# Score-weight loads in two steps, with two small loads moved and a fixed order on SyncE

## The chip, the cores and the metric

The kernel runs on one core of one Trainium2 chip. The metric is the device time of one execution in microseconds; the time shown for a kernel is the median of its runs.

## The reference

There are 128 graphs of 128 nodes with 512 features each, all in float32. Two layers follow each other; each normalizes its input, applies a ReLU, runs a graph layer and adds the result to its input.

```python
# layer 0: graph attention with K = 3 hops
h  = relu(layernorm(x))
Xw = h @ Wv + bv
e  = leaky_relu((Xw @ aw[:d])[:, None, :] + (Xw @ aw[d:])[:, :, None] + ab, 0.2)
t  = adj * exp(e);  t = t / (t.sum(-1, keepdims=True) + 1e-12)
H = 0;  Xk = h
for k in range(3):
    H = H + Xk @ Wk[k] + bk[k];  Xk = t @ Xk
x = x + relu(H)
# layer 1: one attention weight for each node
h = relu(layernorm(x))
q, k = split(h @ Wqk);  v = h @ Wv1
w = (q * (adj @ (k * mask))).sum(-1) * mask / sqrt(512)
x = x + softmax(w, axis=1)[:, :, None] * v
```

## The kernel before

The core works on pairs of graphs, 64 pairs in all. A loop over the pairs does layer 0 and the normalization of layer 1; a second loop over groups of two pairs does layer 1. The large matrix products are cut by Strassen's scheme into seven products of half-size blocks, so TensorE multiplies sums of blocks that VectorE has formed. Ahead of the first loop stands a setup of about 30 us, and the change is there.

**Setup.** The scores of layer 1 need q and k only through one product of them, so the kernel forms the score matrix Wq Wk^T once. The score weights `wqk` (512 x 1024, 2 MB) are loaded into `wqk_sb`, which lies in the tile `tl` (the profile names it `tl`). They come in eight pieces of 256 KB. `oh` is the half of the columns, first or second, of both the q and the k part; `ch` and `c` name the four chunks of 128 rows. Pieces with `c = 0` are issued by SyncE and those with `c = 1` by ScalarE (lines 144 to 150). Then SyncE issues the first pair of graphs (`load_x(0)`, tile `xg`), the attention weights `wv0` (in tile `t10`, named `t`), the second pair, and the three hop weights `wk` (tiles `w2` and `r10`, named `w` and `r`; lines 181 to 187).

GpSimd issues the small loads: the attention vector `awj`, the node mask `nm`, and two parts of the hop biases into `bkj` (lines 155 to 158). It then makes `ident`, the identity that transposes need. A one-element copy `gate` that reads the last piece of the score weights (line 183) holds back the other small loads `bvc`, `awc` and `ab_bc`; a second one that reads `wk[2]` holds back the adjacency loads (`load_adj`, tiles `ag` and `agb`).

TensorE starts with warm-up products on `ones` (`warm`, `warm_whole`, lines 770 to 772), whose results nobody reads. `weights_transposed(ch, oh, banks)` transposes two pieces into two PSUM banks, and ScalarE and VectorE copy them to `wqt` and `wkt`. `score_matrix(f, oh)` multiplies those. TensorE's order is written out by hand: transposes (0, 0), transposes (1, 0), three warm-up products, score matrix (0, 0), transposes (0, 1), masks, score matrix (1, 0), transposes (1, 1), and the rest of the score matrix with the transposes of the first graphs between. The first layer-0 product, `y2(0)`, follows.

VectorE, meanwhile, spreads the attention vector (`aw_bc`), takes the statistics of the first pair (`statistics(xg[0])`: `st`, `mv`, `r`, `rs`), forms the bias columns from `bkj` (`bias_columns`, tile `bkt`), multiplies `wv0` by the attention vector (`attention_columns`, tile `junk`), combines the weights (`combine`) and forms the block sums of the left operand (`left_sums`, tile `sx`).

**Order.** A planner puts the instructions of each engine in order and makes the semaphores for data dependences. `tc.issue_after(ins)`, and the helpers `behind` and `ordered` on it, add an edge of order alone: on `ins`'s engine, what is traced in the block comes later than `ins`, without a wait for its end. `ordered` chains all of TensorE's work.

Of the kernel before, what the change touches and what calls it, by code (L numbers as in the profile page):

```python
# [16 lines left out]
def kernel(  # L17
# [25 lines left out]
    nc = tc.nc  # L43
    B, N, D = x.shape
    K = wk.shape[0]
    P = 128
    DC = D // P
    HC = DC // 2
    HD = D // 2
    G = 2  # L50
    S32 = 32
    Q = P // S32
# [24 lines left out]
    done = {}  # L77

    a1, b1, c1, e1, a2, b2, c2, e2 = (psum.tile([P, D], FP, name=n) for n in
                                      ("a1", "b1", "c1", "e1", "a2", "b2", "c2", "e2"))  # L80
    set1, set2 = (a1, b1, c1, e1), (a2, b2, c2, e2)

    def behind(what, op, *args, **how):

        with tc.issue_after(done[what]):
            return op(*args, **how)  # L86

    def ordered(op, *args, **how):

        with tc.issue_after(done["mm"]):  # L90
            done["mm"] = op(*args, **how).ins  # L91

    def bcast(ap, offset, n):

        return bass.AP(tensor=ap.tensor, offset=ap.offset + offset, ap=[[0, P], [1, n]])

    xg, ag, agb = {}, {}, {}

    def load_x(p, queue=nc.sync):
        xg[p] = loads.tile([P, G, D], FP, name="xg")  # L100
        queue.dma_start(xg[p], x[p * G:(p + 1) * G].rearrange("b n d -> n b d"))

    def load_adj(p):

        s = slice(p * G, (p + 1) * G)
        ag[p] = loads.tile([P, G, N], FP, name="ag", bufs=3)
        nc.sync.dma_start(ag[p], adj[s].rearrange("b n m -> n b m"))
        agb[p] = loads.tile([P, G, Q, S32], FP, name="agb", bufs=2)
        v = adj[s].rearrange("g (q b) (c i) -> c b (g q) i", b=S32, i=S32)
        for c in range(Q):  # L110
            nc.gpsimd.dma_start(agb[p][c * S32:(c + 1) * S32].rearrange("p g q i -> p (g q) i"), v[c])  # L111
# [18 lines left out]
    wqk_sb = tl.rearrange("p t c o -> p (t c o)").rearrange("p (c o) -> p c o", c=DC)  # L130
# [5 lines left out]
    bkj = setup.tile([P, 2, S32], FP, name="bkj")  # L136
# [4 lines left out]
    awc = setup.tile([P, 2, DC], FP, name="awc")  # L141
    bvc = setup.tile([P, DC], FP, name="bvc")

    for oh in range(2):
        for ch in range(2):
            for c in range(HC):
                at = ch * HC + c
                (nc.scalar if c else nc.sync).dma_start(
                    wqk_sb[:, at].rearrange("p (a o) -> p a o", a=2)[:, :, oh * HD:(oh + 1) * HD],
                    wqk[at * P:(at + 1) * P].rearrange("p (a o) -> p a o", a=2)[:, :, oh * HD:(oh + 1) * HD])  # L150
    load_x(0)
    def blocks32(ap, offset, times, n):
        return bass.AP(tensor=ap.tensor, offset=ap.offset + offset, ap=[[0, times], [S32, n], [1, S32]])

    nc.gpsimd.dma_start(awj, blocks32(aw, 0, Q, S32))
    nc.gpsimd.dma_start(nm, nodemask)
    nc.gpsimd.dma_start(bkj[:, 0], blocks32(bk, 0, Q, S32))
    nc.gpsimd.dma_start(bkj[:, 1], blocks32(bk, 2 * D, 2 * Q, D // S32))

    ident = const.tile([P, P], FP, name="ident")  # L160
    make_identity(nc, ident)
# [20 lines left out]
    weights0 = [(wv0_sb, wv0), (r2[:, :, 1:1 + D], wk[2])] + [(r10[:, :, k], wk[1 - k]) for k in range(2)]  # L182
    done["gate"] = nc.gpsimd.tensor_copy(gate, wqk_sb[:, DC - 1, D - 1:D]).ins
    for dst, w in weights0:
        nc.sync.dma_start(dst, w.rearrange("(f p) o -> p f o", p=P))
        if dst is wv0_sb:
            load_x(1)
    with tc.issue_after(done["gate"]):
        nc.gpsimd.dma_start(bvc, bv0.rearrange("(p c) -> p c", c=DC))
        nc.gpsimd.dma_start(awc, aw.rearrange("(a p c) o -> p a (c o)", a=2, c=DC))  # L190
        done["gate"] = nc.gpsimd.dma_start(ab_bc, bcast(ab, 0, 1)).ins
        done["gate"] = nc.gpsimd.tensor_copy(gate, r2[:, DC - 1, D:1 + D]).ins
    load_x(2)

    def spread(dst, col):
# [39 lines left out]
    def warm(times, bank, start=True):  # L235

        for _ in range(times):
            with tc.issue_after(done["mm"]) if "mm" in done else ExitStack():
                done["mm"] = nc.tensor.matmul(bank[:, :P], ones, ones, start=start, stop=True,  # L239
                                              skip_group_check=True).ins  # L240
# [62 lines left out]
    def weights_transposed(ch, oh, banks):  # L303

        for a, bank in enumerate(banks):
            pt = bank.rearrange("p (k n) -> p k n", n=P)
            for c in range(HC):
                for o in range(HC):
                    at = a * D + (oh * HC + o) * P
                    ordered(nc.tensor.transpose, pt[:, o * HC + c if a else c * HC + o, :],  # L310
                            wqk_sb[:, ch * HC + c, at:at + P], ident)
            if a:
                on = "wq" if oh else "wk"
                done[on] = behind(on, nc.scalar.copy if oh else nc.vector.tensor_copy,
                                    wkt[:, oh * HC:(oh + 1) * HC, ch * HD:(ch + 1) * HD],
                                    bank.rearrange("p (o n) -> p o n", o=HC)).ins
            else:
                done["wq"] = behind("wq", nc.scalar.copy,
                                    wqt[:, oh * HC:(oh + 1) * HC].rearrange("p o f c a -> p (o f) c a")[
                                        :, :, ch * HC:(ch + 1) * HC],  # L320
                                    bank.rearrange("p (c o a) -> p o c a", c=HC, a=S32)).ins
# [450 lines left out]
    warm_whole(c2)  # L772
    done["warm"] = done["wk"] = done["wq"] = done["mm"]
    weights_transposed(0, 0, (a2, e2))
    weights_transposed(1, 0, (c1, e1))
    warm(3, b2, False)
    attention_vector_columns()
# [21 lines left out]
    for p in range(2):  # L799
        behind("gate", load_adj, p)  # L800
# [24 lines left out]
    with tc.issue_after(done["hv"]):  # L825
        load_x(3)
        load_adj(2)

    for p in range(NP):
# [4 lines left out]
        elif FIRST <= p < LAST:  # L834
            o, i = divmod(p - FIRST, 4)
# [31 lines left out]
        if LAST < p <= LAST + len(PIECES):  # L867
            o, i = PIECES[p - LAST - 1]
# [45 lines left out]
        if p + 3 < NP:  # L914
            load_adj(p + 3)
# [537 lines left out]
```

## Time and profile before

| quantity | value |
|---|---|
| time, median of 3 runs | 2204.94 us (2204.85 to 2206.91) |
| time of the profiled execution | 2207.55 us |
| its span in the profile | 2205.8 us |
| TensorE busy | 2196.1 us (100%) |
| VectorE, ScalarE, GpSimd busy | 77%, 56%, 35% |
| mean granted TensorE clock | 0.999 |
| moved by DMA | 503.14 MB, mean 228 GB/s |

The span is the time between the first and the last instruction in the profile; the execution's own time is 1.75 us longer. Busy time of TensorE is modelled and pipelined, so 100% says that it hardly ever waits, not that it runs at its peak. PE is TensorE's matrix product, PEld its weight load, DVE VectorE, ACT ScalarE, POOL GpSimd and SP SyncE; a name with a q, such as SPq, is the engine's issue of DMAs. A note in brackets gives the idle time ahead of an instruction and what ended it.

### The profile page before, as it was taken

To read this page: it belongs to the slowest core of one execution; us is meant where nothing else is said; L and a number is where in the kernel's file an instruction comes from. 1 tells how busy PE (TensorE), PEld (TensorE's weight loads), DVE (VectorE), ACT (ScalarE), POOL (GpSimd) and SP (SyncE) were. 2 spreads that over 40 slices of the span, in tenths; PEclk is the share of its full clock that TensorE was granted. 3 is DMA by queue.
4 is the path that set the end of the run, shared out by engine and by line. 5 is a ranking of instruction groups with operands and counts; after the bars stand their busy time and mean duration, and the time that the engine had idled before them with its cause. 6 is when DMAs were issued, how large, how long until landed. Compare 5 with 4: busy or idle time off the path is not lost.

```text
span 2205.8 us, 29518 instructions
## 1 busy us (share of the span) xinstructions
PE 2196.1 (100%) x8113; PEld 1534.7 (70%) x8113; DVE 1697.7 (77%) x4542; ACT 1233.4 (56%) x2856; POOL 778.1 (35%) x951
## 2 busy tenths in 40 slices
PE   9999999999999999999999999999999999999998
PEld 5666666665666666566666666688788878887886
DVE  6778788777878877877877777588777777777777
ACT  4555555555555455555545554466666666666665
POOL 2222222222222222222222222255545554555454
PEclk9999999999999999999999999999999999999999
DMA  6788778777878888887878887868887888787877
GB/s 212 203 227 242 221 237 239 236 245 226 247 226 241 233 237 239 223 246 224 243 220 242 232 231 208 285 181 218 237 224 229 214 236 225 224 218 231 231 212 182
DMA packets 433693, 503.14 MB, mean 228 GB/s; under 512 B 101880, under 2 KB 282104, under 8 KB 429560
## 3 DMA queue, kind: packets, MB, share of 16 engines
q1 hardware_dynamic: 381016, 375.72, 55.9%
q0 software_dynamic: 51136, 123.97, 22.7%
q10 hardware_dynamic: 1376, 1.57, 0.2%
q8 instruction: 65, 1.06, 0.2%
q14 instruction: 100, 0.82, 0.1%
HBM read 287.17 MB, written 213.94 MB: 227 GB/s over the span
## 4 chain that ended last, share of the span: by engine, by line
PE 99%; DVE 0%; DMA 0%; issue 0%; DVEq 0%; ACT 0%
PE a L91 29%; PE c L91 26%; PE b L91 26%; PE e L91 17%; DMA tl<-in_L_gnn_Wqk_dram 0%; DVE c L728 0%; DVE h L728 0%; PE b L239 0%; DVE junk L728 0%; ACT L114 0%; DVEq L1449 0%; PE a L197 0%; DVE x L397 0%; DVE z L86 0%; DVE peak L728 0%
## 5 line engine op out<-in xcount | busy, mean ns | idle before, releaser
L728 POOL TENSOR_TENSOR c<-s,c 128x512 f32<-128x512 f32 (+1 forms) x186 | 201.0, 1093 | 250.6 <-DVE s L728 245.5
L483 POOL DMA_DIRECT2D fd<-fw x124 | 78.4, 636 | 491.6 <-DVE fw L471 459.0
L111 POOL DMA_DIRECT2D agb<-in_adj_dram x256 | 149.4, 590 | 259.1 <-DVE aT L86 238.5
L91 PE MATMUL a<-r,x 128*128 128x512 f32 x512 | 240.8, 592 | 0.0
L91 PE MATMUL b<-rw,in 128*128 128x256 f32 x884 | 212.0, 379 | 0.0
L91 PEld LDWEIGHTS b<-rw,in 128*128 128x128 f32 x884 | 168.0, 190 | 23.3 <-issue 0.5
L91 PEld LDWEIGHTS a<-r,x 128*128 128x128 f32 x512 | 97.2, 190 | 94.8 <-issue 91.1
L86 ACT COPY s<-c 128x257 f32<-128x257 f32 (+1 forms) x128 | 61.6, 481 | 170.3 <-PE c L91 170.3
L86 ACT COPY b<-a 128x257 f32<-128x257 f32 (+1 forms) x128 | 59.4, 464 | 166.8 <-PE a L91 164.2
L728 POOL TENSOR_TENSOR c<-c 128x1024 f32<-128x1024 f32 x61 | 144.1, 2362 | 11.2 <-DVE c L728 10.8
L91 PE MATMUL a<-w,x 128*128 128x257 f32 x512 | 131.9, 380 | 0.1
L91 PE MATMUL b<-w,sx 128*128 128x257 f32 x512 | 132.0, 380 | 0.0
L471 DVE STREAM_TRANSPOSE fw<-hv 128x256 f32<-128x256 f32 x248 | 88.3, 413 | 53.3 <-DMA hv<-h2d 52.2
L91 PE MATMUL c<-t,sx 128*128 128x512 f32 x256 | 120.3, 592 | 0.0
L91 PE MATMUL b<-t,sx 128*128 128x512 f32 x256 | 120.3, 592 | 0.0
L91 PE MATMUL b<-r,sx 128*128 128x512 f32 x256 | 120.3, 592 | 0.0
L91 PE MATMUL e<-t,sx 128*128 128x512 f32 x256 | 120.3, 592 | 0.0
L91 PE MATMUL c<-t,x 128*128 128x512 f32 x256 | 120.3, 592 | 0.0
L728 DVE SCALAR_TENSOR_TENSOR junk<-agg,wscale,c 128x512 f32<-128x512 f32 x126 | 96.2, 763 | 29.4 <-POOL c L728 24.2
L728 ACT ACTIVATE c<-c,wcol 128x512 f32<-128x512 f32 x124 | 86.3, 720 | 55.7 <-DVE wcol L728 55.7
L86 ACT COPY c<-b 128x257 f32<-128x257 f32 (+1 forms) x128 | 59.4, 464 | 99.3 <-PE b L91 99.2
L91 PE MATMUL a<-rw,f 128*128 128x256 f32 x448 | 108.1, 379 | 0.0
(278 smaller groups left out, 5301.2 us busy)
## 6 DMA issues: line engine op xcount, KB each, us to landing
fd<-fw POOLq DMA_DIRECT2D x93, 512.0 KB, 4.7
xg<-in_x_dram SPq DMA_DIRECT2D x64, 512.0 KB, 7.0
x1d<-x SPq DMA_DIRECT2D x64, 512.0 KB, 5.9
h2d<-h SPq DMA_DIRECT2D x64, 512.0 KB, 3.0
hd<-h SPq DMA_DIRECT2D x63, 512.0 KB, 3.0
hv<-hd SPq DMA_DIRECT2D x252, 128.0 KB, 4.2
hv<-h2d SPq DMA_DIRECT2D x248, 128.0 KB, 4.3
h<-h2d SPq DMA_DIRECT2D x62, 512.0 KB, 7.7
```

The costliest lines, as they stand in the source:

```text
L86: return op(*args, **how)
L91: done["mm"] = op(*args, **how).ins
L111: nc.gpsimd.dma_start(agb[p][c * S32:(c + 1) * S32].rearrange("p g q i -> p (g q) i"), v[c])
L471: done["c12"] = nc.vector.transpose(blocks[:, k, j].rearrange("p f (n b) -> p f n b", n=Q), hv[:, j].rearrange("p n (k f a) -> p k f n a", ...
L483: done["fd"] = nc.gpsimd.dma_start(FD[q].rearrange("p o j k n -> p o (j k n)")[:, slots], FW[0].rearrange("p o j k n -> p o (j k n)")[:, s ...
L728: done[engine] = op(*args, **how).ins
```

## The change

The loads of the second column half of the score weights now follow a copy: VectorE copies one column of the first-half piece (`ch = 0`) into the place of the second-half piece of the same chunk, once for `c = 0` and once for `c = 1`. The load of that second-half piece overwrites this column, so it waits for the copy, and the copy waits for the first-half piece. All loads of the setup on SyncE and ScalarE are chained in the order in which they are written. The two `bkj` loads are moved behind the first `gate` copy, ahead of `bvc`. Two more warm-up products are issued between the transposes (0, 0) and (1, 0). `load_adj`'s load on SyncE goes behind the last of the chained loads.

```diff
     def load_x(p, queue=nc.sync):
         xg[p] = loads.tile([P, G, D], FP, name="xg")
-        queue.dma_start(xg[p], x[p * G:(p + 1) * G].rearrange("b n d -> n b d"))
+        done["x"] = queue.dma_start(xg[p], x[p * G:(p + 1) * G].rearrange("b n d -> n b d")).ins
 
     def load_adj(p):
...
-        nc.sync.dma_start(ag[p], adj[s].rearrange("b n m -> n b m"))
+        behind(nc.sync, nc.sync.dma_start, ag[p], adj[s].rearrange("b n m -> n b m"))
...
+    def piece(at, oh):
+        return wqk_sb[:, at].rearrange("p (a o) -> p a o", a=2)[:, :, oh * HD:(oh + 1) * HD]
+
     for oh in range(2):
+        if oh:
+            for c in range(HC):
+                nc.vector.tensor_copy(piece(c, 1)[:, 0, :1], piece(c, 0)[:, 0, :1])
         for ch in range(2):
-            for c in range(HC):
+            for c, queue in enumerate((nc.sync, nc.scalar)):
                 at = ch * HC + c
-                (nc.scalar if c else nc.sync).dma_start(
-                    wqk_sb[:, at].rearrange("p (a o) -> p a o", a=2)[:, :, oh * HD:(oh + 1) * HD],
-                    wqk[at * P:(at + 1) * P].rearrange("p (a o) -> p a o", a=2)[:, :, oh * HD:(oh + 1) * HD])
-    load_x(0)
+                with tc.issue_after(done[queue]) if queue in done else ExitStack():
+                    done[queue] = queue.dma_start(
+                        piece(at, oh),
+                        wqk[at * P:(at + 1) * P].rearrange("p (a o) -> p a o", a=2)[:, :, oh * HD:(oh + 1) * HD]).ins
+    behind(nc.sync, load_x, 0)
+    done[nc.sync] = done["x"]
...
-    nc.gpsimd.dma_start(bkj[:, 0], blocks32(bk, 0, Q, S32))
-    nc.gpsimd.dma_start(bkj[:, 1], blocks32(bk, 2 * D, 2 * Q, D // S32))
...
     for dst, w in weights0:
-        nc.sync.dma_start(dst, w.rearrange("(f p) o -> p f o", p=P))
+        done[nc.sync] = behind(nc.sync, nc.sync.dma_start, dst, w.rearrange("(f p) o -> p f o", p=P)).ins
         if dst is wv0_sb:
-            load_x(1)
+            behind(nc.sync, load_x, 1)
+            done[nc.sync] = done["x"]
     with tc.issue_after(done["gate"]):
+        nc.gpsimd.dma_start(bkj[:, 0], blocks32(bk, 0, Q, S32))
+        nc.gpsimd.dma_start(bkj[:, 1], blocks32(bk, 2 * D, 2 * Q, D // S32))
         nc.gpsimd.dma_start(bvc, bv0.rearrange("(p c) -> p c", c=DC))
...
     weights_transposed(0, 0, (a2, e2))
+    warm(2, b2, False)
     weights_transposed(1, 0, (c1, e1))
```

## The prediction

> **What bounds the kernel now.** I read the page's engine line first, then the chain of waits over the first 80 us, then the timeline and the windows over the stretch that the diff touches. The page says that TensorE is the bound nearly everywhere:
>
> ```profile
> PE 2196.1 (100%) x8113; PEld 1534.7 (70%) x8113; DVE 1697.7 (77%) x4542; ACT 1233.4 (56%) x2856; POOL 778.1 (35%) x951
> ```
>
> The span is 2205.8 us, so TensorE is without work for 9.7 us in all. Whatever the setup saves or loses reaches the end one for one, since behind it TensorE has no slack to absorb it; and no setup change can give more than its own few us. The chain of waits shows where TensorE is late (start us, us, what):
>
> ```profile
> 1.48 7.57 DMA tl<-in_L_gnn_Wqk_dram
> 9.09 0.69 PE c L91 x2
> 9.78 0.85 PE e L91 x4
> 10.64 1.28 PE b L239 x6
> 11.92 2.42 PE a L91 x8
> ```
>
> Up to 9.09 the chain is one transfer: the second 128-row chunk of the second pair of score weights (first half), which the transposes of `weights_transposed(1, 0)` read. The timeline shows both waits on that pair:
>
> ```profile
> 7.96 0.44 PE L91 MATMUL c<-ident,tl 128*128 128x128 f32 x2 [1.62 <-DMA tl<-in_L_gnn_Wqk_dram]
> 9.09 0.69 PE L91 MATMUL c<-ident,tl 128*128 128x128 f32 x2 [0.70 <-DMA tl<-in_L_gnn_Wqk_dram]
> ```
>
> The first pair never shows as a wait: at 4.97 TensorE waited for `ident` from GpSimd. The second half of the weights isn't waited for either (used from 13.3 and 16.0). A second cost follows the wait. Columns: window, length, busy us of PE, PEld, DVE, ACT, POOL, granted clock, DMA share, GB/s:
>
> ```profile
> 5.40:8.80 3.40, 1.37 (x10) 0.89 (x8) 0.69 (x1) 0.59 (x1) 0.00 (x0) 1.00 1.02 294
> 8.80:12.30 3.50, 3.21 (x13) 2.96 (x14) 1.59 (x4) 0.59 (x1) 0.00 (x0) 0.51 1.07 364
> ```
>
> TensorE was busy 40% of the first window, and in the next it ran at half clock.
>
> **What the skill says.** The Trainium skill, "TensorE: Matmul & The Clock Gate", Part 1, says that the clock falls to half after an idle window of about 3.4 us, and keeps to the rule of no idle gap over that length. Here the longest gap was 1.62 us (plus 0.70), and the clock still fell for 3.5 us; the forecast goes by the trace: a half-idle window is enough. "DMA: Bandwidth & Descriptors", Queues, rings and completion order, says that each DMA engine takes one queue's descriptors in ring order. If so, the second half, issued later on the same two queues, was never ahead of the first, and holding it back gives little. The trace can't separate this (294 GB/s in the first window, all engines busy), so I count only part of the possible gain.
>
> **Part by part.**
>
> *Gated second half.* VectorE makes two one-column copies, each after its first piece has landed. The trace has the last of the first pieces there by 5.1 (least time to landing of `tl` 4.3, issued at 0.78). A tiny VectorE copy costs 0.14 to 0.25 us (`c<-ab_bc`, `w<-ucol`); VectorE is idle from 1.0 to 6.37, so it costs nothing. Queued behind the wait: on SyncE the second half, `xg` and all weights of layer 0; on ScalarE two loads (0.55 to 0.88 us to issue each) and then the copy `wqt<-a` of 5.93. So SyncE resumes near 4.3 to 5.2, ScalarE near 5.3, and that copy moves to about 6.6; its reader is the score matrix at 11.7, hence no cost.
>
> *When the first half lands.* By 5.0 us 0.69 MB had moved. Four pieces plus `nm` and `awj` are 1.13 MB; the other 0.44 MB at 294 GB/s would be there at 6.5. That is the lower bound for the piece that now ends the wait at 9.09; 9.09 is the upper. I take 8.2, nearer to no gain, by the ring order and because only the two small `bkj` loads really leave the early traffic: -0.9.
>
> *Two more warm-up matmuls* (`warm(2)`, four passes; four 128-column passes take 0.44) fill TensorE's gap behind 6.33. Busy share of the critical window: 1.37 + 0.44 with nothing landing earlier is 53%; with pieces at about 7.3 and 8.2 it is over 70%. I expect the clock to hold. Worth: from the last piece to the second bank of `weights_transposed(0, 1)` at 14.33 took 5.24. At full clock it is 0.88 (six transposes, by the 0.44 for two after a wait and 0.44 for four), 0.73 for VectorE's copy `wkt<-e`, 0.14 to the score matrix, 1.72 and 0.44: 3.91. So -1.33, and -2.2 with the landing.
>
> *`bkj` moved behind the gate.* This is the part that may cost. Both loads now wait for GpSimd's copy `gate<-tl` (12.66 now, released by the last score-weight piece). VectorE's `bias_columns` stands in its order right behind the statistics of `xg`:
>
> ```profile
> 14.27 0.30 DVE L340 BATCH_NORM_AGGREGATE mv<-st 128x2 f32<-128x6 f32 x2
> 14.48 0.23 DVE L86 STREAM_TRANSPOSE bkt<-bkj 128x64 f32<-128x64 f32 x1
> ...
> 16.13 0.16 DVE L86 TENSOR_TENSOR r<-r 128x2 f32<-128x2 f32 x1 [0.79 <-ACT r L345]
> ```
>
> The last piece lands at L. It is 12.6 now, queued after `xg`; ahead of `xg` it should be earlier, as 2.21 MB, about all eight pieces and the small loads, have moved by 10.0; I take 11.6 (10.7 to 12.6). Then 0.17 for the gate copy, 0.74 for the first `bkj` issue, and issue to landing of the second: its own row has 6.7, its new neighbours have 4.9 to 5.3, `agb` 5.7 in the same traffic. I take 5.3:
>
> ```profile
> bkj<-in_L_gnn_bk_dram POOLq DMA_DIRECT2D x2, 16.0 KB, 6.7
> bvc<-in_L_gnn_bv_dram POOLq DMA_DIRECT2D x1, 2.0 KB, 4.9
> ```
>
> So `bkj` is there at 11.6 + 0.9 + 5.3 = 17.8, and VectorE, which wanted it at 14.5 or earlier, stands. Queued behind: the end of the statistics, so `h` on ScalarE and its transposes, the eight `junk` products of `attention_columns`, the combinations of `w`, and `sx`. Slack in the old timing: 0.79 (the wait at 16.13) plus the time from the first `sx` (ends 25.40) to its product's weights:
>
> ```profile
> 24.98 0.42 DVE L413 TENSOR_TENSOR sx<-x 128x256 f32<-128x256 f32 x1
> ...
> 29.14 0.84 PEld L91 LDWEIGHTS e<-w,sx 128*128 128x128 f32 x4
> ```
>
> That is 3.74, together 4.53: with `bkj` at 14.48 + 4.53 = 19.0 TensorE keeps its old time, so this path gives 17.8 - 19.0 = -1.2. Over `h` (0.79, 0.95 in ScalarE, 3.2 to its transpose at 22.03) the limit is 19.4, so `sx` decides. The later of the two paths (-2.2 from the front, -1.2 from `bkj`) sets the time: **-1.2 us**. `bvc`, `awc` and `ab` shift by the 1.39 us that the two `bkj` issues take, less the earlier gate; used at 22.95 and 29.0 against 17.7, 18.7 and 19.2 landed, no cost unless L passes 14.
>
> *Fixed order on SyncE, `load_adj` behind it.* The order is what the trace has: score weights, `xg`, `wv0`, `xg`, `wk`. Nothing. `xg` (waited for at 13.06) has the same bytes ahead of it; anything up to 1 us either way is inside the 3.4 us that `bkj` makes VectorE stand. `wk[2]` landed by 20.25 and is read at 22.75; the layer-0 loads start behind a queue that stays full, so no cost, and 1 us of lateness would be covered by VectorE's own.
>
> **Sum.** Profiled 2207.55 - 1.2 = 2206.3 (span 2204.6); the median of the runs is 2.6 lower than that execution, so 2204.94 - 1.2 = **2203.7**.
>
> **Rivals and chances.** A measurement tells about 0.2% (4.4 us) from no change.
>
> - Forecast (0.50): front gain cut back by the `bkj` wait; own range -2.2 to +0.2 (`bkj` at 16.5 to 19.2).
> - `bias_columns` gets another place in VectorE's order, or `bkj` lands by 16.8 (0.22): the full -2.2, 2202.7. For: VectorE's order is made by a planner that takes what is ready; against: the diff leaves its edge on the statistics.
> - The change doesn't do what it says (0.13): ring order already served the first half first, the piece lands at 9.1 and the clock falls anyway: 2204.9. For: the page above; against: `warm(2)`.
> - Slower (0.15): the `bkj` wait decides. Place: VectorE behind `mv`, now at 14.5. From a landing after 19.0 each us there is a us at the end. With L = 12.6 and `bkj`'s own 6.9 it is 12.6 + 0.9 + 6.9 = 20.4: +1.4, 2206.3. For: its own row; against: that row had `nm`'s 64 KB ahead in the same queue.
>
> Past 0.2% on the slow side needs `bkj` at 23.4, on the fast side more than the front holds (6.5 for the piece gives 2.6 + 1.33 = 3.9). So within 0.2% gets 0.89, slower 0.06, faster 0.05, these for a shift in the loop's order that no row shows. Range 2201.5 to 2206.8: from the second case to past the fourth, with about 1 us for the runs' own spread (2204.85 to 2206.91).
>
> **What would show it.** Right: the last `c<-ident,tl` near 8.2, no half-clock window after it, `gate<-tl` near 11.6, an idle gap of 3 us or more ahead of `bkt<-bkj` released by a DMA, `e<-w,sx` near 28. Wrong: `bkt` without a wait; a clock of 0.5 after 8.8; the last piece still at 9.1; or idle time of TensorE in the loop.

## The result, and the profile after

The changed kernel takes 2209.49 us (median of 17 runs, 2208.49 to 2210.47) against 2204.99 us of the kernel before (17 runs beside them, 2204.4 to 2208.1): a ratio of 1.0018, interval 1.0011 to 1.0026. A second series gave 2209.51 (20 runs), ratio 1.0016, interval 1.0009 to 1.0023. So the change costs about 4 us. That is just under the 0.2% which the forecast took as the least that can be told from no change, but both intervals lie above 1. The ratio is the one on record with the runs and isn't the quotient of the two medians (which lie 4.5 us apart here). The forecast had 2203.7 with a range to 2206.8: the sign was wrong, and the result lies outside the range.

The page's engine line shows four more TensorE products (the two warm-ups, two passes each), two more VectorE instructions (the column copies), and little change in the sums:

```profile
PE 2195.6 (99%) x8117; PEld 1533.4 (69%) x8117; DVE 1701.7 (77%) x4544; ACT 1232.2 (56%) x2856; POOL 777.8 (35%) x951
```

The span is 2206.9 us, so TensorE is without work for 11.3 us instead of 9.7. The chain of waits over the first 80 us (start us, us, what; only the longest pieces are listed) shows where:

```profile
0.78 4.09 DMA tl<-in_L_gnn_Wqk_dram
5.08 0.55 ACTq L155
5.67 7.10 DMA tl<-in_L_gnn_Wqk_dram
13.00 0.64 POOL bkj L196
13.64 5.85 DMA bkj<-in_L_gnn_bk_dram
21.32 0.62 DVE junk L270 x2
```

Before, this chain went through one transfer of the first half and then stayed on TensorE. Now it goes first half, issue on ScalarE, second half, GpSimd's `bkj` issue, the `bkj` transfer, and then VectorE. None of the pieces listed up to 21 us is TensorE's own work. The same steps in the timeline (start us, us, engine, line, operation; in brackets the idle time before and what ended it):

```profile
7.23 0.66 PE L91 MATMUL c<-ident,tl 128*128 128x128 f32 x4 [1.00 <-DMA tl<-in_L_gnn_Wqk_dram]
12.82 0.18 POOL L189 COPY gate<-tl 128x1 f32<-128x1 f32 x1 [8.77 <-DMA tl<-in_L_gnn_Wqk_dram]
13.75 0.30 DVE L349 BATCH_NORM_AGGREGATE mv<-st 128x2 f32<-128x6 f32 x2
19.59 0.24 DVE L86 STREAM_TRANSPOSE bkt<-bkj 128x64 f32<-128x64 f32 x1 [5.54 <-DMA bkj<-in_L_gnn_bk_dram]
22.22 0.66 PE L91 MATMUL a<-ident,h 128*128 128x128 f32 x4 [2.34 <-ACT h L374]
29.16 0.42 DVE L422 TENSOR_TENSOR sx<-x 128x256 f32<-128x256 f32 x1
29.63 0.73 PEld L91 LDWEIGHTS e<-w,sx 128*128 128x128 f32 x4 [0.43 <-DVE sx L422]
```

A row such as the first, with x4, holds the products on the last two pieces of the first half. Those on the last piece start inside it, at 7.51, which is 1.6 us earlier than in the profile before (9.09). TensorE gives the gain back twice: it waits 2.34 us for `h`, and the first layer-0 product waits for `sx`, because VectorE stood 5.54 us for `bkj` ahead of `bkt`. It starts at 29.63, against 29.14 before. The clock did hold (windows; busy us of PE, PEld, DVE, ACT, POOL, granted clock, DMA share, GB/s):

```profile
4.80:8.20 3.40, 2.39 (x20) 2.10 (x20) 0.85 (x2) 0.86 (x2) 0.00 (x0) 1.00 0.95 275
8.20:11.60 3.40, 3.19 (x18) 2.02 (x17) 2.11 (x4) 0.31 (x1) 0.00 (x0) 1.00 1.02 330
```

TensorE is busy 70% of the first of these windows, and the second is at full clock. The row of the DMA view (issues, KB each, median us from issue to landing) puts `bkj` at 5.8:

```profile
bkj<-in_L_gnn_bk_dram POOLq DMA_DIRECT2D x2, 16.0 KB, 5.8
```

All of the difference lies in the setup. From the weights of the first `e<-t,sx` (a layer-0 product that comes after `y2(0)`; 36.57 before, 37.73 after) to the end of the span it is 2169.2 us in both profiles, and within 0.1 us of that in all eleven profiles below.

### The profile page after: what moved, and what is told of

Read it like the earlier page. It is cut to its first block, busy times and chain, and to the rows that moved or that the text cites. A ratio compares the mean times of both kernels' runs of the same rounds, so it can differ in the third digit from the quotient of the medians.

```text
span 2206.9 us, 29529 instructions
## 1 busy us (share of the span) xinstructions
PE 2195.6 (99%) x8117; PEld 1533.4 (69%) x8117; DVE 1701.7 (77%) x4544; ACT 1232.2 (56%) x2856; POOL 777.8 (35%) x951
## 4 chain that ended last, share of the span: by engine, by line
PE 98%; DVE 1%; DMA 1%; ACT 0%; issue 0%; POOL 0%; DVEq 0%; ACTq 0%
PE a L91 29%; PE b L91 26%; PE c L91 26%; PE e L91 17%; DMA tl<-in_L_gnn_Wqk_dram 1%; DMA bkj<-in_L_gnn_bk_dram 0%; DVE junk L270 0%; DVE c L737 0%; DVE w L211 0%; DVE h L737 0%; ACT h L374 0%; DVE junk L737 0%; DVE st L348 0%; ACT ej L737 0%; PE a L206 0%
## 5 line engine op out<-in xcount | busy, mean ns | idle before, releaser
L737 POOL TENSOR_TENSOR c<-c 128x1024 f32<-128x1024 f32 x61 | 144.1, 2362 | 11.3 <-DVE c L737 10.9
```

The source lines that it names most:

```text
L737: done[engine] = op(*args, **how).ins
```

## The experiments

**The kernel before, again.** The two profiles differ by 1.1 us in span and the medians by 4.5, so before anything else I wanted to know what one execution of the old kernel is worth. It ran twice more without an edit.

> The kernel before, once more, to see how typical its profiled execution is: that one took 2207.55 us, 2.6 over the median of its runs, and had a half-clock window of 3.4 us (8.9 to 12.3). Theory (the bkj wait explains the whole loss, measured against an execution in which TensorE ran earlier): most executions have no such window, so a profile near 2205 us shows TensorE's product e<-w,sx starting about 2.5 us earlier than 29.1, near 26.6. Rival (the profile is typical and the loss beyond 1.2 us arises in the loop): the window and 29.1 come again, and a profile near 2205 has its shorter time in the loop.

The first gave 2205.33 us (13 runs, 2204.28 to 2207.6), ratio 0.9998, interval 0.999 to 1.0006. Its profiled execution took 2206.76; the last piece was used at 8.19, and here too TensorE's clock fell, although it was busy for 51% of the window before (windows, columns as above):

```profile
4.80:8.20 3.40, 1.73 (x12) 1.07 (x11) 0.69 (x1) 0.59 (x1) 0.57 (x5) 1.00 0.96 298
8.20:11.60 3.40, 3.40 (x13) 2.94 (x14) 1.80 (x4) 0.59 (x1) 0.00 (x0) 0.50 1.08 347
```

> A third profile of the kernel before. If it takes 2204 to 2205.5, it has no half-clock window and TensorE's e<-w,sx starts near 26.7; if it takes 2206.5 or more, it has the window and a start at 28.3 or later.

The second is a single execution of 2204.64 (span 2202.8). It is close to the old kernel's median, and its timeline is another one:

```profile
7.03 0.66 PE L91 MATMUL c<-ident,tl 128*128 128x128 f32 x4 [0.58 <-DMA tl<-in_L_gnn_Wqk_dram]
13.53 0.23 DVE L86 STREAM_TRANSPOSE bkt<-bkj 128x64 f32<-128x64 f32 x1
26.20 0.84 PEld L91 LDWEIGHTS e<-w,sx 128*128 128x128 f32 x4
33.64 0.19 PEld L91 LDWEIGHTS e<-t,sx 128*128 128x128 f32 x1 [0.24 <-DVE t L202]
```

Here the products on the last piece start at 7.31, no window of the setup is at half clock, and `e<-w,sx` starts at 26.20 instead of 29.14. The front gain that the prediction hoped for, and more, is in this execution without any edit. The old kernel's runs spread widely. In the three series of experiments they have medians of 2205.21, 2206.09 and 2205.01 and run from 2204.08 to 2210.29, 50 of 123 over 2206.2. Each run has its mean granted clock, rounded: the 21 runs at 1.000 took at most 2206.43, the 20 runs at 0.998 or less at least 2208.39, so the slowest runs lost clock. The other 82 stand at 0.999 and take 2204.3 to 2208.65, and 29 of the 50 long runs are among them. There the rounded figure tells nothing: a window of 3.4 us at half clock is 0.0008 of the mean, and the executions of 2207.55 with such a window and of 2204.64 without one both show 0.999. Lost clock isn't all of it either: in two profiles below the last piece is late (8.96 and 8.97), the clock holds, and the time is 2206.36 and 2206.34. The first profile, at 2207.55, had both, and was one of the longer ones.

**`bkj` back in its place.** The changed kernel with only its `bkj` loads moved back ahead of `ident`.

```diff
     nc.gpsimd.dma_start(nm, nodemask)
+    nc.gpsimd.dma_start(bkj[:, 0], blocks32(bk, 0, Q, S32))
+    nc.gpsimd.dma_start(bkj[:, 1], blocks32(bk, 2 * D, 2 * Q, D // S32))
...
     with tc.issue_after(done["gate"]):
-        nc.gpsimd.dma_start(bkj[:, 0], blocks32(bk, 0, Q, S32))
-        nc.gpsimd.dma_start(bkj[:, 1], blocks32(bk, 2 * D, 2 * Q, D // S32))
```

> The changed kernel with the two bkj loads back at their first place (ahead of ident, not behind the gate); gating, fixed order and warm-up stay. Theory (bkj wait): VectorE's wait of 5.5 us ahead of bkt<-bkj goes and the time falls to 2203.5 to 2206, equal to before within 1 us. Rival 1 (the gated loads land later and delay VectorE or the loop): it stays at 2208 to 2210. Rival 2 (half and half): 2206.5 to 2207.5.

2205.13 us (13 runs, 2204.75 to 2205.97), ratio to before 0.9996, interval 0.9988 to 1.0004. The whole loss is gone, as expected. Its timeline:

```profile
11.59 0.44 PE L91 MATMUL a<-ident,tl 128*128 128x128 f32 x2 [0.55 <-DMA tl<-in_L_gnn_Wqk_dram]
13.53 0.23 DVE L86 STREAM_TRANSPOSE bkt<-bkj 128x64 f32<-128x64 f32 x1
26.84 0.84 PEld L91 LDWEIGHTS e<-w,sx 128*128 128x128 f32 x4
```

`bkt` has no wait, and `e<-w,sx` is 2.79 us earlier than in the changed kernel. It is also 2.3 us earlier than in the profile before, which is the -2.2 that the prediction worked out for the front, and still the median is where it was. The first row is a wait that the gating can bring: a second-half piece is now waited for, 0.55 us.

**`bkj` late, alone.** The kernel before with nothing but the `bkj` loads behind the gate: the reverse of the diff above, on the other kernel.

> The kernel before with one edit: the two bkj loads behind the gate copy. Theory (bkj wait): all of the loss, 2208 to 2211, with bkt<-bkj released by a DMA near 19.5. Rival 1 (gated loads): 2204.5 to 2205.5, no change. Rival 2: about 2207.

2207.74 us (21 runs, 2207.17 to 2209.33), ratio 1.0007, interval 1.0001 to 1.0014. The expectation had all of the loss, 2208 to 2211, and it is less. Its timeline:

```profile
11.93 0.18 POOL L181 COPY gate<-tl 128x1 f32<-128x1 f32 x1 [7.87 <-DMA tl<-in_L_gnn_Wqk_dram]
18.36 0.25 DVE L86 STREAM_TRANSPOSE bkt<-bkj 128x64 f32<-128x64 f32 x1 [5.12 <-DMA bkj<-in_L_gnn_bk_dram]
28.40 0.73 PEld L91 LDWEIGHTS e<-w,sx 128*128 128x128 f32 x4 [0.43 <-DVE sx L413]
```

The late `bkj` is enough for a loss: about 2.5 us by the medians, 1.5 by the ratio. From `bkt` to `e<-w,sx` it takes 10.04 us, to the hundredth what it takes in the changed kernel (19.59 to 29.63): VectorE's queue sets the time in both, and the changed kernel is later by the 1.23 us that its `bkt` is later. Of these, 0.89 are the gate copy (12.82 against 11.93) and 0.34 the transfer (5.85 against 5.51 in the two chains).

**The bias columns later.** The changed kernel with `bkj` left late, but `bias_columns`, which reads it, moved in VectorE's order behind `combine` of the hop weights.

```diff
     h0_rs = behind("wk", statistics, xg[0], "wq")
-    behind("aggr", bias_columns)
     weights_transposed(1, 1, (a2, e2))
...
         right2 = combine(halves(r2, W2), [t2[:, i] for i in range(4)])
+    behind("right", bias_columns)
```

> The changed kernel, all of it, but VectorE's bias_columns goes behind the combinations of the layer-0 weights and so behind the place where anyone waits for it (bias_a and bias_e are read at about 33). The bkj loads stay late. Theory (it is VectorE's place in the queue, not the loads, that costs): 2203.5 to 2206, as with the early loads or up to 1 us better. Rival 1 (gated loads): 2208 to 2210.

2205.3 us (13 runs, 2204.43 to 2205.7), ratio 0.9997, interval 0.9989 to 1.0006. Its timeline:

```profile
25.50 0.24 DVE L86 STREAM_TRANSPOSE bkt<-bkj 128x64 f32<-128x64 f32 x1
26.90 0.84 PEld L91 LDWEIGHTS e<-w,sx 128*128 128x128 f32 x4
```

The load is still behind the gate (13.63 here), and nothing waits for it. So it isn't the traffic of the late `bkj` that costs, it is the place of its reader in VectorE's order.

**The warm-ups alone, the gating alone.** The kernel before with `warm(2)` only; the changed kernel without `warm(2)` and with `bkj` early, which leaves the gating and the fixed order on SyncE together.

```diff
     weights_transposed(0, 0, (a2, e2))
+    warm(2, b2, False)
     weights_transposed(1, 0, (c1, e1))
```

> The kernel before plus the two warm-up matmuls alone. So far the kernel before ran from 2204.1 to 2209.5 and both its profiles held a half-clock window of 3.4 us in the setup, while the two changed kernels without the bkj wait ran from 2204.4 to 2206.0 with no window. Theory A (the upper part of the spread of before is that window, and the warm-up matmuls prevent it): 2204.4 to 2205.5 median, no run over 2206.5, no window in the profile. Theory B (it is the gating that narrows the spread, because the first half lands earlier): the spread stays, some runs at 2207 to 2209.

> The changed kernel without its two warm-up matmuls and with the bkj loads at their first place: gating and fixed order alone. Theory A (warm-up matmuls prevent the window): the spread of before comes back, some runs at 2206.5 to 2209. Theory B (gating narrows it): all runs within 2204.4 to 2206, last c<-ident,tl near 7. Either way gating alone costs a wait of about 0.5 us for the gated pieces at 11.6.

Beside these the kernel before had 2206.09 (33 runs). The warm-ups gave 2205.0 (13 runs, 2204.55 to 2208.51), ratio 0.9997, interval 0.9989 to 1.0005, with 6 of 13 over 2206.2 (16 of 33 for the kernel before): the spread stayed. The gating gave 2205.14 (2204.59 to 2206.05), ratio 0.9994, interval 0.9985 to 1.0002, with none of 13 over 2206.2. The timeline of the warm-ups alone, and then of the gating alone, at the last pieces of the first half:

```profile
8.96 0.44 PE L91 MATMUL c<-ident,tl 128*128 128x128 f32 x2 [1.20 <-DMA tl<-in_L_gnn_Wqk_dram]
```

```profile
7.66 0.66 PE L91 MATMUL c<-ident,tl 128*128 128x128 f32 x4 [1.18 <-DMA tl<-in_L_gnn_Wqk_dram]
```

With the warm-ups the last piece can still be late, and in this execution (2206.36) the clock held all the same; with the gating both pieces are there at 7.66, and the products on the last start at 7.94. In the six profiles without gating they start between 7.31 and 9.09; in the seven with gating, between 7.12 and 7.94. The gating does what the change says. It narrows the spread and hardly moves the median, since an execution near the median already has the early piece. What the fixed order on SyncE has in this wasn't separated. The wait of about 0.5 us for a gated piece, which was expected of this kernel too, isn't in its profile.

**No gating, bias columns later.** The kernel before with `warm(2)`, `bkj` late and `bias_columns` moved as above; the loads of the second half stay ungated.

> The kernel before with the bkj loads late, bias_columns behind the weight combinations, and the two warm-up matmuls; no gating, no fixed order. It has ident 1.4 us earlier, nothing waiting for bkj and no wait for a gated piece. If gating is what costs the 0.5 us wait at 11.6 in the two kernels without the bkj wait, this is the best version: 2203.8 to 2204.8. If gating brings a gain of its own (first half earlier), it is 2205 to 2206 or spread like before.

2206.14 us (13 runs, 2204.1 to 2207.89), ratio 0.9997, interval 0.9989 to 1.0005, 5 of 13 over 2206.2; in its profile the last piece is used at 8.97. The expectation had it as the best version, at 2203.8 to 2204.8, if gating only costs; it isn't. Taking `bkj` out of the early traffic doesn't bring the first half forward by itself, and the spread stays without the gating.

**One gate for both queues.** Both column copies read the piece that SyncE loaded, so ScalarE's second-half loads no longer wait for ScalarE's own first piece; first with `bias_columns` late, then with `bkj` early.

```diff
-                nc.vector.tensor_copy(piece(c, 1)[:, 0, :1], piece(c, 0)[:, 0, :1])
+                nc.vector.tensor_copy(piece(c, 1)[:, 0, :1], piece(0, 0)[:, 0, :1])
```

> The kernel with late bias columns (gating, fixed order, warm-up, bkj late, bias_columns behind the combinations), with both column copies reading the one piece that SyncE loads first; ScalarE's second-half load no longer waits for ScalarE's own first piece. That kernel had TensorE wait 0.55 us at 11.65 for the gated piece of ScalarE; first pieces landed about 0.8 us apart. Theory (gating keeps the spread small, its price is this wait): the wait goes, 2204.3 to 2205.0, all runs below 2206. Rival (starting ScalarE's load earlier undoes the gating): the last first-half piece lands at 8 or later in some runs, which reach 2206.5 or more.

> The changed kernel with the bkj loads at their first place and the same one piece for both copies. Theory: like the kernel with early bkj loads (2205.1) or up to 0.6 us better, 2204.5 to 2205.2, no wait at 11.6. Rival: some runs at 2206.5 or more.

2204.93 us (13 runs, 2204.47 to 2205.29), ratio 0.9993, interval 0.9985 to 1.0001, and 2205.22 (13 runs, 2204.73 to 2206.01), ratio 0.9996, interval 0.9988 to 1.0004. The timeline of the first:

```profile
11.14 0.60 PE L91 MATMUL a<-ident,tl 128*128 128x128 f32 x4
26.55 0.84 PEld L91 LDWEIGHTS e<-w,sx 128*128 128x128 f32 x4
```

There is no wait for a second-half piece, and `e<-w,sx` is 0.35 us earlier than with two gates. That the one gate did this isn't shown: the gating alone, with two gates, had no such wait either, and with `bkj` early the one gate gains nothing (2205.22 against 2205.13). Of the versions run, the first has the lowest median: 4.6 us under the changed kernel. Against the kernel before its median can't be told from the same. Its runs all lie within 0.8 us, where those of the kernel before spread over 5 us, and so its mean is 2204.87 against 2205.86 beside it.

**The changed kernel, again.**

> The changed kernel once more beside these. Theory (TensorE's time is set by the landing of the second bkj load): 2208.5 to 2210.5, and in its profile e<-w,sx starts 10.0 us behind the start of bkt<-bkj, and e<-t,sx 8.1 us behind that, whatever the landing. Rival (something else limits too): these distances differ by more than 0.3 us from those of the two profiles with late bkj loads.

2209.51 us (20 runs, 2208.16 to 2210.81). Its profiled execution took 2210.02, 1.3 more than the first profile of this kernel (2208.7). The timeline, and then three windows behind it:

```profile
20.22 0.24 DVE L86 STREAM_TRANSPOSE bkt<-bkj 128x64 f32<-128x64 f32 x1 [6.31 <-DMA bkj<-in_L_gnn_bk_dram]
22.85 0.66 PE L91 MATMUL a<-ident,h 128*128 128x128 f32 x4 [2.83 <-ACT h L374]
31.55 0.84 PEld L91 LDWEIGHTS e<-w,sx 128*128 128x128 f32 x4
```

```profile
20.80:24.20 3.40, 1.30 (x9) 1.06 (x10) 3.12 (x14) 2.22 (x4) 3.31 (x6) 1.00 1.04 380
24.20:27.60 3.40, 3.40 (x6) 1.38 (x5) 3.26 (x9) 0.82 (x3) 1.36 (x3) 0.51 1.11 304
27.60:31.00 3.40, 3.40 (x9) 1.44 (x9) 3.40 (x15) 1.09 (x2) 0.00 (x0) 0.99 0.23 41
```

`bkj` is 0.63 us later than in the first profile. TensorE stands 2.83 us for `h`, is busy 38% of that window, and runs the next one at half clock, in the middle of the score matrix. `e<-w,sx` has no wait ahead of it any more: TensorE itself is late. The rival in the expectation came true here: from `bkt` to `e<-w,sx` it is 11.33 us instead of 10.0, and `e<-t,sx` (38.99) follows after 7.44 instead of 8.1. Up to `e<-t,sx` this execution is 1.26 us behind the first profile: 0.63 for the later `bkj` and 0.63 behind it. So the change, which was to hold the clock at 8.9, can lose it at 24.2.

How busy TensorE was doesn't by itself tell when the clock falls. The first profile of the changed kernel, over its own wait for `h`, and then the kernel without gating and with late bias columns, over its wait for the last pieces:

```profile
19.60:23.00 3.40, 1.01 (x6) 0.49 (x6) 3.09 (x14) 1.65 (x3) 1.93 (x4) 1.00 1.05 365
23.00:26.40 3.40, 3.40 (x11) 1.76 (x12) 3.23 (x11) 1.90 (x4) 2.93 (x6) 1.00 1.06 353
```

```profile
5.60:9.00 3.40, 1.25 (x11) 0.82 (x8) 0.69 (x1) 0.51 (x1) 0.00 (x0) 1.00 1.00 326
9.00:12.40 3.40, 3.19 (x16) 2.14 (x17) 2.12 (x4) 0.58 (x1) 0.00 (x0) 1.00 1.06 383
```

TensorE is busy 30% and 37% of these windows, less than in the two windows of the old kernel after which the clock fell, and the clock stays full.

## Why the prediction was wrong

**The mechanism was named, on the wrong side.** The account had the path through the `bkj` wait ahead of `bkt`, and the rival "slower" said that this wait decides. It does: `bkj` early, or its reader later, takes away all of the loss, and `bkj` late alone makes a loss. What failed is the sizes, and one step above all.

**The failed step: the baseline in the "Sum", and with it the limit of 19.0.** I measured the gain and the slack in one execution that took 2207.55 and carried both over to a median 2.6 us lower, as if the difference had nothing to do with the steps. It had much to do with them. That execution had a late piece (9.09) and a half-clock window; an execution near the median (2204.64) has the piece at 7.31 and no such window. So the -2.2 of the front, true against the profile, is nothing against the median: with `bkj` early the front is 2.3 us ahead of that profile, and the ratio is 0.9996. The slack is smaller too. VectorE needs 10.04 us from `bkt` to `e<-w,sx`, and in the execution near the median that product starts at 26.20, so the limit for `bkj` is 26.20 - 10.04 = 16.2 and not 19.0. With the forecast's own landing of 17.8 the sum would have read +1.6.

**The landing, 17.8 in the step "`bkj` moved behind the gate".** It was 19.5: the gate at 12.82 instead of 11.6 (1.2) and 5.85 instead of 5.3 for the transfer (0.55). I had the last score-weight piece come earlier because it goes ahead of `xg`. But the gating starts it later: in the chain its transfer runs from 5.67, once the first piece has landed and VectorE has copied, against 4.11 in the chain of `bkj` late alone. The gate copy runs at 11.79 to 13.63 in the seven gated profiles and at 11.93 to 12.87 in the six others. The two ranges overlap; nothing shows the 1 us gain that was assumed.

**A term left out.** Behind `sx` VectorE is still late, and a second wait follows, which the text didn't speak of. In the changed kernel's timeline:

```profile
33.18 0.14 DVE L86 COPY c<-ab_bc 128x1 f32<-128x1 f32 x1
33.37 0.52 PEld L91 LDWEIGHTS c<-ccol,ones 128*128 128x128 f32 x4 [0.41 <-DVE c L86]
37.73 0.19 PEld L91 LDWEIGHTS e<-t,sx 128*128 128x128 f32 x1 [0.24 <-DVE t L211]
```

From `e<-w,sx` to `e<-t,sx` it takes 8.10 us here and with `bkj` late alone, against 7.43 or 7.44 in the kernel before and with `bkj` early: 0.67 more. `ab_bc` isn't what is late: VectorE has run without a pause from `bkt` on and comes to this copy at 33.18.

**The account.** Against the execution near the median: 29.63 - 26.20 = 3.43 for the later `bkt`, and 0.67 behind it, 4.1 in all; the spans differ by 2206.9 - 2202.8 = 4.1. The medians differ by 4.5. The rest may be executions with a half-clock window at 24.2 like the one of 2210.02, but how often it comes isn't counted in the traces. By the mean clocks of the second series, the 7 runs at 0.998 took 2209.39 to 2210.49 and the 4 at 1.000 took 2208.34 to 2209.31, which fits it; but in the first series 6 runs at 0.998 (2209.07 to 2210.47) and 6 at 1.000 (2208.7 to 2210.09) overlap, so it stays open.

In the forecast's own terms the miss of 5.8 us comes apart like this. Against the profile that it measured in, `e<-w,sx` was to start at 27.94 and starts at 29.63: 1.7 for the landing. The second wait behind it is 0.67. The step from the profiled execution to the median is the other 3.4: 2.6 were taken off, while the changed kernel's median lies 0.8 above its own profiled execution (2208.7).

**What held.** The last piece earlier (7.51, forecast 8.2, lower bound 6.5) and full clock at 8.9, which isn't shown to be the change's doing, as the old kernel's 2204.64 has both; the gap of 3 us or more ahead of `bkt` released by a DMA (5.54); `sx` as the path and not `h`; the column copies, the fixed order on SyncE and `load_adj` at no visible cost. With `bkj` early these parts together leave the median at 0.9996 (0.9988 to 1.0004). The price of the "slower" rival, +1.4, was set from a limit of 19.0; with `bkj` at 19.5 it would have given only +0.5.

**The ring order and the idle window.** The first half landed in a narrower and earlier band when the second was held back (7.12 to 7.94 against 7.31 to 9.09). That is the opposite of what I drew from the ring order told of in "DMA: Bandwidth & Descriptors", which made me discount the gating. The same section of the Trainium skill also says that completion is not first in, first out, since a later descriptor may finish its write before an earlier one. That may be the reason, but no run here separates the reads from the writes.

Three profiles of one unchanged kernel have half clock at 8.9, at 8.2 and not at all. "TensorE: Matmul & The Clock Gate", Part 1, says that the activity window is free-running and that cold products vary from run to run, and the three profiles agree. I read only the rule on idle windows, and the forecast's reading that a half-idle window is enough doesn't hold as a rule: two windows at 30% and 37% above went by at full clock.

## What to carry to other kernels

Compare the profiled execution's own time with the median first: if it is longer by as much as the change may be worth, take another profile near the median and find out what the excess is, because a gain that only removes that excess doesn't move the median. A load that is moved behind a gate is dear by what stands behind its first reader in that engine's order, not by its bytes; move the reader as well, which here took the 4 us away. And look for the gain of a steadier start in the spread of the runs, not in their middle.

## What was not expected of the hardware

- TensorE's clock fell to half after windows in which it was busy 38%, 40% and 51% of 3.4 us, with no idle gap over 2.83 us. It held after windows at 30%, 37%, 65% (gating alone) and 70%. The lost windows are cut where the fall begins, the others anywhere, so no bound on the busy share follows.
- The unchanged kernel's last first-half piece is used at 7.31, 8.19 or 9.09. With the second half held back on the same two queues, and the order on SyncE fixed, it is 7.12 to 7.94, and where VectorE doesn't wait for `bkj` no run is over 2206.1 (65 runs of five kernels, against 50 of 123 over 2206.2 for the kernel before).
- The 16 KB `bkj` load took 4.5 us from issue to landing when issued early beside the gated loads, and 5.8 and 6.2 behind the gate in the two profiles of the changed kernel (medians of its two issues).
